# GAT tails that take both halves of the batches at once, and one output array: a four-layer graph network on one core

## The chip, the cores and the metric

The kernel runs on one core of a Trainium2 chip. A core has TensorE (PE, whose weight loads are listed as PEld), VectorE (DVE), ScalarE (ACT), GpSimd (POOL) and SyncE (SP), which work side by side, each through its own queue of instructions in order, and 16 DMA engines. The metric is the device time of one execution in microseconds (us); the median of several runs is quoted. Of one execution there is a profile: the start and length of every instruction, what ended the idle time before it, and the transfers.

## The reference

There are 8 batches of 2048 nodes with 128 features, and one adjacency matrix for all of them, with about 0.8% of its entries set. Four layers follow each other on the same x. Layers 0 and 1 are attention with 8 heads of 16 features over the neighbours, a residual and a layer norm, a feed-forward part of 256 and another residual and norm. The change doesn't touch these. Layers 2 and 3 are single-head graph attention (GAT):

```python
h = x @ W
e = leaky_relu(h @ a_src [:, None] + h @ a_dst [None, :], slope=0.2)
e = where(adj == 0, -inf, e)
out = softmax(e, axis=-1) @ h
y = out + x
x = ln_gamma * (y - mean(y)) * rsqrt(var(y) + 1e-5) + ln_beta
```

## The kernel before

**Tiles.** The nodes are sorted by the number of their neighbours and cut into 16 tiles of 128 nodes, one node per partition. Tile t handles up to 30, 23, 21, 20, 19, 18, 18, 17, 16, 16, 15, 14, 14, 13, 12, 11 neighbours per node, for t = 0 to 15. For each layer a table in DRAM holds one row per node with the projected features of all 8 batches and the attention terms (4 KB and a little more for layers 2 and 3). `gather` fetches one neighbour's row for each of a tile's 128 nodes with one indirect DMA that POOL issues (L320), so a tile of 20 neighbours takes 20 such instructions. They go to one of six buffers called kv, in chunks of 2 neighbours (layers 0 and 1) or 4 (layers 2 and 3).

**A chunk of a GAT layer** (`gat_chunk`). DVE makes the weights (L745, L746, L751) and multiplies the gathered rows of six batches by them (L757); ACT multiplies those of the last two batches (L762). DVE then adds the two halves of the chunk (L766), and PE accumulates the result in PSUM (L772). L766 needs both L757 and L762. After the last chunk of a tile, DVE divides by the sum of the weights and writes `o` (L649).

**The tail of a tile** (`gat_tail`). It runs twice per tile, once for batches 0 to 3 and once for batches 4 to 7. PE adds `o`, the residual and a constant row in PSUM (L782 to L790). `normed` then does the norm: ACT squares each batch's row and sums it up (L471), POOL raises the four sums of a node to the power of -0.5 (L476, 128 x 4 elements), and ACT scales by that (L480). The mean is taken out by the weights. For layer 2, PE transposes the result (L329), ACT copies it, and `project` makes the half row of layer 3's table, in a tile called rows. When the second half is done, `state_done` stores x and writes the 128 rows into the table with an indirect DMA from POOL (`put_rows`, L494), and counts it in `put`. For layer 3, DVE multiplies by gamma (L807) and adds beta (L808), and POOL writes the half tile to the output with an indirect DMA (L810, 256 KB). There are two output arrays, one for each four batches, which the host puts together.

**Order.** The order of the instructions on each engine is that in which the program emits them; no scheduler moves anything. `layers` goes through all chunks of all layers. For each chunk it calls `slot` three times, and a slot advances every running side thread and every tail by one step (to its next `yield`) and then lets `fetch` issue further gathers, up to 3 or 4 chunks ahead of the one at work. The two tails of a tile start 1 and 4 slots after `o` is written. So a tail's power lands in POOL's queue between the gathers of later chunks, and its squares and scales land in ACT's queue between the multiplies L762 of later chunks.

**Layer boundaries.** The gathers of a layer need the whole table, which the last tile of the layer before completes. To shorten that wait, the lists of tiles 0 and 1 are sorted so that some of their chunks need only the table without its last three, two or one tiles; `fetch` issues those as soon as `put` says so. A table write waits for the gathers of that table that are under way, and the gathers behind it wait for it to land.

**Buffers.** The half tiles of the norm are in a pool of two (tag n), the rows tile has one buffer, and the PSUM tiles of the tails come from a pool of three (`misc`).

Of the kernel before, what the change touches and what calls it, by code (L numbers as in the profile page):

```python
# [8 lines left out]
F32 = mybir.dt.float32  # L9
# [4 lines left out]
AF = mybir.ActivationFunctionType  # L14
# [68 lines left out]
def sparse_path(ctx: ExitStack, tc: tile.TileContext, ins: dict, out: bass.AP, flag: bass.AP):  # L83
# [19 lines left out]
    def misc():  # L103
        return pm.tile([P, 512], F32, tag="m", name="m")
# [12 lines left out]
    half = const.tile([P, 4], F32, name="half")  # L117
    nc.vector.memset(half, -0.5)

    spread = const.tile([P, P], F32, name="spread")  # L120
# [344 lines left out]
    def normed(z, dst):  # L465

        yield

        ss = small.tile([P, 4], F32, tag="ss", name="ss", bufs=3)
        for i in range(4):  # L470
            nc.scalar.activation(  # L471
                dst[:, i, :], z[:, i, :], AF.Square, bias=eps, scale=D**-0.5,
                accum_out=ss[:, i : i + 1],
            )
        rs = small.tile([P, 4], F32, tag="rs", name="rs", bufs=3)
        nc.gpsimd.tensor_tensor(rs, ss, half, op=ALU.pow)  # L476
        yield
        yield
        for i in range(4):
            nc.scalar.mul(dst[:, i, :], z[:, i, :], rs[:, i : i + 1])  # L480
        yield
# [18 lines left out]
    def project(l, i, xT, rows, t):  # L500

        w = W[l]
        if l < 2:
            for h in range(0, 4, 2):
                pp = misc().rearrange("p (b c) -> p b c", c=2 * D)
                if w["bias"] is not None:
                    nc.tensor.matmul(
                        pp, ones_bf, w["bias"][:, None, D:].to_broadcast([P, 2, 2 * D]),
                        start=True, stop=False, skip_group_check=True,
                    )  # L510
                for j in range(2):
                    nc.tensor.matmul(
                        pp[:, j, :], xT[:, i + h + j, :], w["qkv"][:, D:],
                        start=w["bias"] is None and j == 0, stop=True, skip_group_check=True,
                    )
                yield
                at = (i + h) * 2 * D
                nc.scalar.copy(rows[:, at : at + 512], pp.rearrange("p b c -> p (b c)"))  # L518
        else:
            pp = misc().rearrange("p (b c) -> p b c", c=D)  # L520
            nc.tensor.matmul(
                pp, ones_bf, w["bias"][:, None, :D].to_broadcast([P, 4, D]),
                start=True, stop=False, skip_group_check=True,
            )
# [22 lines left out]
            nc.scalar.copy(score[:, l - 2, t, 2 * i : 2 * i + 8], ps.rearrange("p b c -> p (b c)"))  # L547
# [106 lines left out]
    def rows_of(box):  # L654
        if "rows" not in box:
            box["rows"] = work.tile([P, NB * 2 * D], F32, tag="rows", name="rows", bufs=1)
        return box["rows"]
# [117 lines left out]
                )  # L775
        yield

    def gat_tail(l, t, box, i):
        wt = W[l]
        xT = box["x"]  # L780
        y = misc().rearrange("p (b c) -> p b c", c=D)
        nc.tensor.matmul(  # L782
            y, ones_bf, wt["row_z"][:, None, :].to_broadcast([P, 4, D]),
            start=True, stop=False, skip_group_check=True,
        )
        nc.tensor.matmul(
            y, ident, box["o"][:, i : i + 4, :], start=False, stop=False, skip_group_check=True
        )
        for j in range(4):
            nc.tensor.matmul(  # L790
                y[:, j, :], xT[:, i + j, :], wt["res1"], start=False, stop=True,
                skip_group_check=True,
            )
        n2 = work.tile([P, 4, D], F32, tag="n", name="n2")
        yield from normed(y, n2)
        if l == 2:
            pt = transpose4(n2)
            yield
            nc.scalar.copy(xT[:, i : i + 4, :], pt)
            yield  # L800
            yield from project(3, i, xT, rows_of(box), t)
            yield
            state_done(l, t, box)
        else:
            for _ in range(4):
                yield
            nc.vector.tensor_mul(n2, n2, last_g[:, None, :].to_broadcast([P, 4, D]))  # L807
            nc.vector.tensor_add(n2, n2, last_b[:, None, :].to_broadcast([P, 4, D]))  # L808
            yield
            nc.gpsimd.indirect_dma_start(  # L810
                out=out[i // 4],
                out_offset=bass.IndirectOffsetOnAxis(ap=perm[:, t : t + 1], axis=0),
                in_=n2.rearrange("p b d -> p (b d)"), in_offset=None,
            )
            state_done(l, t, box)


# [203 lines left out]
    for l in range(4):  # L1021
        per = 2 if l < 2 else 4
        for t, k, ns, folded in pieces(l, per):
# [2 lines left out]
            c["run"] = (attention_chunk if l < 2 else gat_chunk)(l, c)  # L1026
            every.append(c)
    now = [0, 0]

    def advance(group):  # L1030
        for g in list(group):
# [27 lines left out]
    def drain():  # L1059
        while threads or tails:  # L1060
# [93 lines left out]


@with_exitstack
def general_path(ctx: ExitStack, tc: tile.TileContext, ins: dict, outs: list):

# [444 lines left out]
    for b in range(B):  # L1603
        x = x_next
        if b + 1 < B:
            x_next = load_x(b + 1)
        attention(x, W[0])
        attention(x, W[1])
        gat(x, W[2])
        gat(x, W[3])  # L1610
        o = outs[b // 4][:, (b % 4) * D : (b % 4 + 1) * D]
        nc.sync.dma_start(o.rearrange("(t p) d -> p t d", p=P), x)


# [64 lines left out]
```

## Time and profile before

| what | us |
| --- | --- |
| median of 3 runs | 3421.49 |
| lowest and highest | 3416.98, 3424.4 |
| profiled execution | 3421.15 |
| its span | 3419.3 |
| DVE busy | 3063.5 (90%) |
| PE busy | 2746.3 (80%) |
| POOL busy | 2213.2 (65%) |
| ACT busy | 1429.0 (42%) |

The span is the time from the first to the last instruction; 1.85 us of the execution lie around it. The 16 DMA engines moved 986.52 MB, 289 GB/s on average. The four layers overlap little, and each has its own limits, so the shares over the whole span must not be read as those of the part in question. Layer 2 begins at about 2300 us and layer 3 at about 2840 us, and both are shorter than the layers before them. In a line of the groups, "out<-in" names the tiles, then comes the count, the busy time and the mean, and after the second bar the idle time of that engine just before these instructions and what ended it.

### The profile page before, as it was taken

Reading aid. Unit: us, or ns where it says so; the run is one execution under the profiler, and the core shown is the slowest. Engines: PE = TensorE matmul, PEld = TensorE weight load, DVE = VectorE, ACT = ScalarE, POOL = GpSimd, SP = SyncE. Lnnn points to the kernel's source line nnn. Section 1 sums busy time; section 2 is a strip of 40 time slices with the busy share of each in tenths; the row PEclk is TensorE's granted clock in tenths of the full one; section 3 lists DMA queues with packets and bytes.
Section 4 is the critical chain, followed back from the end, with each engine's and each line's share of the span. In section 5 each row is a group of like instructions: output and inputs, shape, how many; then the busy total and the mean of one; then the engine's idle time right before and its main releaser. Section 6 shows DMA issues by size and latency. Waiting matters only on the chain.

```text
span 3419.3 us, 34694 instructions
## 1 busy us (share of the span) xinstructions
PE 2746.3 (80%) x10618; PEld 1585.2 (46%) x10618; DVE 3063.5 (90%) x2727; ACT 1429.0 (42%) x4972; POOL 2213.2 (65%) x1501
## 2 busy tenths in 40 slices
PE   5647888888989997788888999985888976667775
PEld 4523445445555653455545555642444543233332
DVE  7789999999999989999999999965888876788885
ACT  5711333334444541233334344443555654344444
POOL 0065788688667655465676756646788865688873
PEclk9878999999999999999999999987999997889888
DMA  8487877888888777687887887757999986789883
GB/s 340 181 333 266 300 284 282 314 299 291 307 305 311 279 265 285 229 328 282 318 323 291 300 307 277 283 184 267 334 337 349 346 307 241 276 296 319 297 286 123
DMA packets 200881, 986.52 MB, mean 289 GB/s; under 512 B 32174, under 2 KB 33968, under 8 KB 128692
## 3 DMA queue, kind: packets, MB, share of 16 engines
q0 software_dynamic: 175280, 890.45, 71.8%
q1 hardware_dynamic: 20502, 75.52, 5.7%
q10 hardware_dynamic: 4904, 18.24, 1.4%
q8 instruction: 87, 1.43, 0.2%
q14 instruction: 108, 0.88, 0.1%
HBM read 937.16 MB, written 91.55 MB: 301 GB/s over the span
## 4 chain that ended last, share of the span: by engine, by line
DVE 34%; PE 23%; issue 18%; DMA 10%; POOL 6%; ACT 3%; POOLq 0%; DVEq 0%; ACTq 0%
DVE kv L620 12%; DVE kv L606 12%; PE acc L630 7%; PE acc L772 6%; DMA kv<-table,lists 5%; POOL kv L320 4%; DVE sc L609 2%; DVE kv L757 2%; DMA kv<-table,sorted_lists 2%; DVE kv L766 2%; PE m L712 2%; DVE sums L455 1%; DMA table<-rows,perm 1%; PE m L329 1%; PE m L691 1%
## 5 line engine op out<-in xcount | busy, mean ns | idle before, releaser
L320 POOL DMA_INDIRECT kv<-table,lists x955 | 1422.8, 1490 | 352.6 <-issue 205.8
L630 PE MATMUL acc<-kv,ident 128*128 128x512 f32 x2200 | 1107.2, 633 | 229.4 <-DVE kv L620 229.2
L772 PE MATMUL acc<-kv,ident 128*128 128x512 f32 x1184 | 618.2, 672 | 203.0 <-DVE kv L766 155.6
L630 PEld LDWEIGHTS acc<-kv,ident 128*128 128x128 f32 x2200 | 413.9, 202 | 663.1 <-issue 367.5
L606 DVE TENSOR_TENSOR kv<-kv,q 128x2048 f32<-128x2048 f32 (+1 forms) x282 | 629.4, 2232 | 18.9 <-DMA kv<-table,lists 10.1
L609 DVE TENSOR_REDUCE sc<-kv 128x128 f32<-128x2048 f32 (+1 forms) x284 | 634.0, 2233 | 9.2
L620 DVE TENSOR_TENSOR kv<-kv,w 128x2048 f32<-128x2048 f32 (+1 forms) x284 | 631.5, 2224 | 8.2 <-ACT w L615 7.4
L476 POOL TENSOR_TENSOR rs<-ss,half 128x4 f32<-128x4 f32 x192 | 290.5, 1513 | 422.6 <-ACT n L471 421.1
L471 ACT ACTIVATE n<-m,eps 128x128 f32<-128x128 f32 x768 | 271.9, 367 | 568.7 <-PE m L712 216.7
L772 PEld LDWEIGHTS acc<-kv,ident 128*128 128x128 f32 x1184 | 243.4, 216 | 508.2 <-issue 299.4
L757 DVE TENSOR_TENSOR kv<-kv,pair 128x3072 f32<-128x3072 f32 (+1 forms) x150 | 466.3, 3108 | 1.0
L766 DVE TENSOR_TENSOR kv<-kv 128x2048 f32<-128x2048 f32 (+1 forms) x150 | 296.2, 1975 | 147.3 <-ACT kv L762 147.3
L762 ACT ACTIVATE kv<-kv,ws 128x128 f32<-128x128 f32 x1108 | 339.4, 406 | 146.3 <-DVE ws L751 118.9
L480 ACT ACTIVATE n<-m,rs 128x128 f32<-128x128 f32 x768 | 219.6, 370 | 371.5 <-POOL rs L476 371.2
L615 ACT ACTIVATE w<-sc,lmask 128x64 f32<-128x64 f32 x554 | 164.9, 351 | 457.6 <-DVE sc L609 457.0
L320 POOL DMA_INDIRECT kv<-table,sorted_lists x153 | 199.9, 1307 | 114.5 <-PE acc L630 47.6
L494 POOL DMA_INDIRECT table<-rows,perm x57 | 106.5, 1868 | 110.2 <-ACT rows L518 26.4
L329 PE MATMUL m<-ident,n 128*128 128x128 f32 x640 | 106.9, 289 | 85.3 <-ACT n L480 85.3
L471 ACT ACTIVATION_READ_ACCUMULATOR n<-m,eps 128x1 f32 x768 | 157.4, 205 | 0.0
L712 PE MATMUL m<-w_L_w,hT 128*128 128x128 f32 x1024 | 156.4, 275 | 0.0
L329 PEld LDWEIGHTS m<-ident,n 128*128 128x128 f32 x640 | 81.5, 146 | 142.2 <-ACT n L480 92.7
L712 PEld LDWEIGHTS m<-w_L_w,hT 128*128 128x128 f32 x1024 | 135.2, 192 | 0.0
(234 smaller groups left out, 3237.8 us busy)
## 6 DMA issues: line engine op xcount, KB each, us to landing
kept<-xT SPq DMA_DIRECT2D x48, 512.0 KB, 7.6
xT<-kept SPq DMA_DIRECT2D x48, 512.0 KB, 6.4
kv<-in_adj_dram SPq DMA_DIRECT2D x16, 1024.0 KB, 6.4
table<-kv ACTq DMA_DIRECT2D x16, 1024.0 KB, 4.3
kv<-table,lists POOLq DMA_INDIRECT x955, 7.0
kv<-in_x_nodes_dram SPq DMA_DIRECT2D x16, 512.0 KB, 6.6
kv<-table,sorted_lists POOLq DMA_INDIRECT x153, 6.2
found<-cand POOLq DMA_DIRECT2D x16, 64.0 KB, 4.1
```

The costliest lines, as they stand in the source:

```text
L320: nc.gpsimd.indirect_dma_start(out=dst, out_offset=None, in_=tables[l][:, :], in_offset=bass.IndirectOffsetOnAxis(ap=index, axis=0), bound ...
L471: nc.scalar.activation(dst[:, i, :], z[:, i, :], AF.Square, bias=eps, scale=D**-0.5, accum_out=ss[:, i : i + 1],)
L476: nc.gpsimd.tensor_tensor(rs, ss, half, op=ALU.pow)
L606: nc.vector.tensor_mul(kk, kk, q[:, None].to_broadcast([P, ns, NB, D]))
L609: nc.vector.tensor_reduce(sc[:, :ns].rearrange("p s (b h) -> p (s b) h", h=NH), kk.rearrange("p s b (h j) -> p (s b) h j", h=NH), axis=AX. ...
L620: nc.vector.tensor_mul(vv, vv, w[:, k : k + ns, :].rearrange("p s (b h) -> p (s b) h", h=NH)[:, :, None, :] .to_broadcast([P, ns * NB, HD, ...
L630: nc.tensor.matmul(acc[:, j, :], merge if c["folded"] else ident, kv[:, i, 4 * j : 4 * j + 4, D:], start=k + i == 0, stop=c["last"] and i ...
L712: nc.tensor.matmul(y[:, j, :], hT[:, f, j, :], wt["2"][:, f, :], start=False, stop=f == 1, skip_group_check=True,)
L757: nc.vector.tensor_mul(hv[:, :, :nv, :], hv[:, :, :nv, :], wc[:, :, :nv, None].to_broadcast([P, ns, nv, D]))
L762: nc.scalar.mul(hv[:, i, b, :], hv[:, i, b, :], ws[:, i, b - nv : b - nv + 1])
L766: nc.vector.tensor_add(hv[:, : ns - left], hv[:, : ns - left], hv[:, left:ns])
L772: nc.tensor.matmul(acc[:, j, :], merge if c["folded"] else ident, hv[:, i, 4 * j : 4 * j + 4, :], start=k + i == 0, stop=c["last"] and i = ...
```

## The change

A GAT tail now takes both halves. It adds both in PSUM, squares the first half, squares the second, and calls one power of 128 x 8 elements. In layer 2 the halves then go on one by one, the second two slots behind the first, to the same table write. In layer 3 both halves are written into the tile that was the table's rows (one buffer), gamma and beta are applied to all 128 x 1024 elements in one instruction each, and one indirect DMA of 512 KB writes them to one output array of 2048 rows of 8 x 128; the host transposes it. The steps between are laid out anew in slots. Besides, `slot` advances the tails a second time in every third slot as long as the chunk at work is one of the last tile of layer 2, or is one of layers 2 or 3 whose table is not yet complete. Layers 0 and 1 keep their own tails with a power of 128 x 4, and are affected only in that `half` is now 8 wide.

```diff
-    def gat_tail(l, t, box, i):
+    def gat_tail(l, t, box):
         wt = W[l]
         xT = box["x"]
...
-        n2 = work.tile([P, 4, D], F32, tag="n", name="n2")
-        yield from normed(y, n2)
+        if l == 2:
+            ns = [work.tile([P, 4, D], F32, tag="n", name="n2") for _ in range(2)]
+        else:
+            n = rows_of(box)[:, : B * D].rearrange("p (b d) -> p b d", d=D)
+            ns = [n[:, :4, :], n[:, 4:, :]]
+        ys = [None, None]
+        ss = small.tile([P, 8], F32, tag="ss", name="ss", bufs=3)
+        rs = small.tile([P, 8], F32, tag="rs", name="rs", bufs=3)
...
+        def half_rows(h):
+            scaled(h)
+            yield
+            pt = transpose4(ns[h])
+            yield
+            nc.scalar.copy(xT[:, 4 * h : 4 * h + 4, :], pt)
+            yield
+            yield from project(3, 4 * h, xT, rows_of(box), t)
+            yield
+            state_done(l, t, box)
+
+        added(0)
+        yield
+        squares(0)
+        added(1)
+        yield
+        squares(1)
+        nc.gpsimd.tensor_tensor(rs, ss, half, op=ALU.pow)
+        for _ in range(3):
+            yield
         if l == 2:
-            pt = transpose4(n2)
-            yield
-            nc.scalar.copy(xT[:, i : i + 4, :], pt)
-            yield
-            yield from project(3, i, xT, rows_of(box), t)
-            yield
-            state_done(l, t, box)
+            parts = [half_rows(0), later(2, lambda: half_rows(1))]
+            while parts:
+                advance(parts)
+                yield
         else:
-            for _ in range(4):
-                yield
-            nc.vector.tensor_mul(n2, n2, last_g[:, None, :].to_broadcast([P, 4, D]))
-            nc.vector.tensor_add(n2, n2, last_b[:, None, :].to_broadcast([P, 4, D]))
+            scaled(0)
+            yield
+            scaled(1)
+            for _ in range(3):
+                yield
+            nc.vector.tensor_mul(n, n, last_g[:, None, :].to_broadcast([P, B, D]))
             yield
+            nc.vector.tensor_add(n, n, last_b[:, None, :].to_broadcast([P, B, D]))
+            yield
             nc.gpsimd.indirect_dma_start(
-                out=out[i // 4],
-                out_offset=bass.IndirectOffsetOnAxis(ap=perm[:, t : t + 1], axis=0),
-                in_=n2.rearrange("p b d -> p (b d)"), in_offset=None,
+                out=out, out_offset=bass.IndirectOffsetOnAxis(ap=perm[:, t : t + 1], axis=0),
+                in_=n.rearrange("p b d -> p (b d)"), in_offset=None,
             )
             state_done(l, t, box)
...
+    def hurry():
+        c = every[min(now[0], len(every) - 1)]
+        return c["l"] == 2 and c["t"] == NT - 1 or c["l"] > 1 and put[c["l"]] < NT
+
     def slot():
         advance(threads)
         advance(tails)
         fetch()
+        beat[0] += 1
+        if beat[0] % 3 == 0 and hurry():
+            advance(tails)
...
-        part = attention_tail if l < 2 else gat_tail
-        tails.append(later(1, lambda: part(l, t, box, 0)))
-        tails.append(later(4, lambda: part(l, t, box, 4)))
+        if l < 2:
+            tails.append(later(1, lambda: attention_tail(l, t, box, 0)))
+            tails.append(later(4, lambda: attention_tail(l, t, box, 4)))
+        else:
+            tails.append(later(1, lambda: gat_tail(l, t, box)))
```

The inner functions `added`, `squares` and `scaled` hold the same instructions as the tail and `normed` did, for half h.

More of the change, by code (lines that the diff above doesn't have):

```diff
@@ L116, in sparse_path @@
     nc.vector.memset(onesc, 1.0)
-    half = const.tile([P, 4], F32, name="half")
+    half = const.tile([P, 8], F32, name="half")
     nc.vector.memset(half, -0.5)
@@ L475, in normed @@
         rs = small.tile([P, 4], F32, tag="rs", name="rs", bufs=3)
-        nc.gpsimd.tensor_tensor(rs, ss, half, op=ALU.pow)
+        nc.gpsimd.tensor_tensor(rs, ss, half[:, :4], op=ALU.pow)
         yield
@@ L776, in gat_chunk, with added @@
         yield
-    def gat_tail(l, t, box, i):
+    def gat_tail(l, t, box):
         wt = W[l]
         xT = box["x"]
[L781 to L789, printed above, removed]
-            nc.tensor.matmul(
-                y[:, j, :], xT[:, i + j, :], wt["res1"], start=False, stop=True,
+        if l == 2:
[6 more added lines that the diff above has]
+        rs = small.tile([P, 8], F32, tag="rs", name="rs", bufs=3)
+        def added(h):
+            ys[h] = y = misc().rearrange("p (b c) -> p b c", c=D)
+            nc.tensor.matmul(
+                y, ones_bf, wt["row_z"][:, None, :].to_broadcast([P, 4, D]),
+                start=True, stop=False, skip_group_check=True,
+            )
+            nc.tensor.matmul(
+                y, ident, box["o"][:, 4 * h : 4 * h + 4, :], start=False, stop=False,
@@ L792, in gat_tail, with squares @@
                 skip_group_check=True,
             )
-        n2 = work.tile([P, 4, D], F32, tag="n", name="n2")
-        yield from normed(y, n2)
-        if l == 2:
-            pt = transpose4(n2)
+            for j in range(4):
+                nc.tensor.matmul(
+                    y[:, j, :], xT[:, 4 * h + j, :], wt["res1"], start=False, stop=True,
+                    skip_group_check=True,
+                )
+        def squares(h):
+            for j in range(4):
+                nc.scalar.activation(
+                    ns[h][:, j, :], ys[h][:, j, :], AF.Square, bias=eps, scale=D**-0.5,
+                    accum_out=ss[:, 4 * h + j : 4 * h + j + 1],
+                )
@@ L798, in gat_tail, with scaled @@
+        def scaled(h):
+            for j in range(4):
+                at = 4 * h + j
+                nc.scalar.mul(ns[h][:, j, :], ys[h][:, j, :], rs[:, at : at + 1])
+        def half_rows(h):
+            scaled(h)
             yield
-            nc.scalar.copy(xT[:, i : i + 4, :], pt)
+            pt = transpose4(ns[h])
             yield
-            yield from project(3, i, xT, rows_of(box), t)
+            nc.scalar.copy(xT[:, 4 * h : 4 * h + 4, :], pt)
+            yield
+            yield from project(3, 4 * h, xT, rows_of(box), t)
@@ L802, in gat_tail @@
             yield
             state_done(l, t, box)
-        else:
-            for _ in range(4):
+        added(0)
[7 more added lines that the diff above has]
+            yield
+        if l == 2:
+            parts = [half_rows(0), later(2, lambda: half_rows(1))]
+            while parts:
+                advance(parts)
+                yield
+        else:
+            scaled(0)
+            yield
+            scaled(1)
+            for _ in range(3):
@@ L1028, in sparse_path @@
     now = [0, 0]
+    beat = [0]
     def advance(group):
@@ L1156, in general_path @@
 @with_exitstack
-def general_path(ctx: ExitStack, tc: tile.TileContext, ins: dict, outs: list):
+def general_path(ctx: ExitStack, tc: tile.TileContext, ins: dict, out: bass.AP):
     nc = tc.nc
@@ L1610, in general_path @@
         gat(x, W[3])
-        o = outs[b // 4][:, (b % 4) * D : (b % 4 + 1) * D]
+        o = out[:, b * D : (b + 1) * D]
         nc.sync.dma_start(o.rearrange("(t p) d -> p t d", p=P), x)
@@ L1663 @@
         ).ap()
-    outs = [
-        nc.dram_tensor(f"out_{i}_dram", [N, 4 * D], F32, kind="ExternalOutput").ap()
-        for i in range(B // 4)
-    ]
+    out = nc.dram_tensor("out_dram", [N, B * D], F32, kind="ExternalOutput").ap()
     with tile.TileContext(nc) as tc:
@@ L1670 @@
             flag = fp.tile([1, 1], I32, name="flag")
-            sparse_path(tc, aps, outs, flag)
+            sparse_path(tc, aps, out, flag)
             bad = nc.values_load(flag[:1, :1], min_val=0, max_val=P)
             with tc.If(bad > 0):
-                general_path(tc, aps, outs)
+                general_path(tc, aps, out)
     r = run_bass_kernel_spmd(nc, [arrays], core_ids=[0])
-    got = r.results[0]
-    halves = [got[f"out_{i}_dram"].reshape(N, 4, D).transpose(1, 0, 2) for i in range(B // 4)]
-    return np.ascontiguousarray(np.concatenate(halves, axis=0))
+    got = r.results[0]["out_dram"]
+    return np.ascontiguousarray(got.reshape(N, B, D).transpose(1, 0, 2))
```

## The prediction

> **What bounds the kernel now.** I first split the span into the stretches that the change touches, then read for each what GpSimd (POOL) does, then who waits for it. The windows view, cut by hand at the layer boundaries (columns: stretch, its length, busy time of PE, PEld, DVE, ACT, POOL, granted clock, DMA share, GB/s):
>
> ```profile
> 2210.00:2350.00 140.00, 99.53 (x453) 62.30 (x451) 81.28 (x68) 62.96 (x236) 64.76 (x56) 0.85 0.54 190
> 2350.00:2770.00 420.00, 358.50 (x1356) 201.60 (x1357) 358.19 (x383) 234.65 (x924) 339.18 (x273) 0.94 0.95 343
> 2770.00:2900.00 130.00, 84.56 (x311) 47.80 (x310) 82.22 (x81) 55.07 (x216) 70.53 (x58) 0.80 0.69 243
> 2900.00:2975.00 75.00, 48.15 (x119) 21.50 (x117) 56.14 (x63) 24.80 (x96) 49.77 (x40) 0.86 0.80 280
> 2975.00:3350.00 375.00, 267.18 (x650) 120.21 (x650) 320.48 (x359) 172.53 (x653) 300.28 (x237) 0.87 0.88 300
> ```
>
> These are the boundary from layer 1 to 2, layer 2's steady part, the boundary from 2 to 3, layer 3's first tiles and its steady part. Layers 0 and 1 before them are not edited. At the boundaries everything is half idle. In layer 2 the DMA share is 0.95, so at most 5% of 420, 21 us, can be won there. Layer 3 has slack on every engine at first sight. The groups of instructions on POOL in that last window (count, busy us, mean ns, idle before):
>
> ```profile
> L320 POOL DMA_INDIRECT kv<-table,lists x192 | 244.4, 1273 | 56.1 <-issue 39.0 <-PE acc L772 7.5 <-DMA kv<-table,lists 3.4
> L810 POOL DMA_INDIRECT out_dram<-n,perm x22 | 33.2, 1509 | 6.7 <-issue 4.0 <-DVE kv L757 1.2 <-DVE ws L751 0.6
> L476 POOL TENSOR_TENSOR rs<-ss,half 128x4 f32<-128x4 f32 x23 | 25.6, 1114 | 18.0 <-ACT n L471 17.7
> ```
>
> POOL is idle 375 - 300.28 = 74.7 us, but 17.7 of that is the power waiting for squares, and nearly all the rest is 0.2 to 0.3 us between two instructions. It hardly waits for a free buffer: its queue is always full. The waits of the same window (total, times, longest):
>
> ```profile
> ACT n L480 <- POOL rs L476: 83.9, 23, 11.6
> DVE kv L766 <- ACT kv L762: 57.9, 17, 10.0
> ACT n L471 <- DMA out_dram<-n,perm: 45.7, 10, 9.2
> ```
>
> DVE, busy 320 of 375, waits for one thing only: the multiplies that ACT does for two batches (L762). These stand in ACT's queue behind the scaling (L480), which waits for the power, which stands in POOL's queue among gathers. So the loop is: full POOL queue, late power, late ACT, late DVE. A POOL instruction saved is worth its time until DVE's 57.9 us are gone. The timeline of POOL in the first tiles of layer 3 and at the boundary before it shows two other places:
>
> ```profile
> 2951.35 1.03 POOL L810 DMA_INDIRECT out_dram<-n,perm  x1 [0.30 <-issue]
> 2958.54 1.04 POOL L476 TENSOR_TENSOR rs<-ss,half 128x4 f32<-128x4 f32 x1 [6.17 <-ACT n L471]
> ...
> 2966.83 1.03 POOL L810 DMA_INDIRECT out_dram<-n,perm  x1 [0.30 <-issue]
> 2973.99 1.03 POOL L476 TENSOR_TENSOR rs<-ss,half 128x4 f32<-128x4 f32 x1 [6.13 <-ACT n L471]
> ```
>
> ```profile
> 2812.54 1.05 POOL L494 DMA_INDIRECT table<-rows,perm  x1 [5.95 <-DMA kv<-table,sorted_lists]
> ...
> 2821.71 1.05 POOL L476 TENSOR_TENSOR rs<-ss,half 128x4 f32<-128x4 f32 x1
> ...
> 2863.33 2.96 POOL L494 DMA_INDIRECT table<-rows,perm  x1 [9.79 <-ACT score L547]
> ```
>
> In the first, a power waits for squares that wait for a scatter of the output to land, because they write the tile it reads. In the second, tile 14's second power starts at 2821.71 although its squares ended at 2811.4 (ACT's timeline): it stands behind four gathers, which wait for the table write of 2812.54 to land. The table's last write, 2863.33, opens layer 3.
>
> **What the Trainium skill says.** "SBUF — State Buffer", section "Who interferes with whom": a DVE instruction with two SBUF inputs contends with a GpSimd instruction that reads SBUF, and whoever is first holds the port pair throughout. The trace agrees:
>
> ```profile
> 3067.55 2.28 DVE L766 TENSOR_TENSOR kv<-kv 128x2048 f32<-128x2048 f32 x1
> 3067.65 3.10 POOL L320 DMA_INDIRECT kv<-table,lists  x1 [0.30 <-issue]
> ```
>
> A gather takes 1.00 us alone (3065.01) and 3.10 here. Hence the means above 1.0, and each POOL instruction removed can also take a collision with it. "DMA: Bandwidth & Descriptors", section "Anatomy of one DMA — SWDGE (gpsimd) path", prices a transfer at 2.0 us plus bytes at 436 GB/s: 2.6 us for 256 KB, 3.2 for 512 KB. The trace is slower, 5.2 us median from issue to landing for the 256 KB scatter; I keep its 5.2 and add 256 KB at the 343 GB/s seen, 0.75. "GPSIMD Engine Reference", section "3.1 Elementwise — side-by-side cycle accounting", gives about 2.6 cycles per element for a two-input operation. Four more columns would then cost an estimated 0.01 us; but the page does not price a power, and the trace has 1.04 us for four columns where a one-column memset takes 0.10. So the page is no guide here.
>
> **The change, part by part.** The unknown is the power of 128x8. Lower bound 1.04 us (all fixed), upper bound 0.10 + 2 x 0.94 = 2.0 (all but the memset's 0.10 grows with the columns). I take the middle, 1.5. The squares, scales, adds and projections keep their number (8 squares take 2 x 1.45 = 2.9 us, 8 scales 2 x 1.14 = 2.3). The two halves of the scatter become one of 512 KB with the same 128 rows, so I keep 1.5 us for its issue on POOL.
>
> 1. Boundary 1 to 2. Now the second power of tile 13 (2290.15) stands behind eight gathers that waited for the write at 2275.84, and ACT waits 7.71 us for it. The instruction order has a merged power ahead of the next table write, and the extra advance of the tails brings it earlier. Later work of tile 14 fills part. Gain 5 us, bounds 0 and 12.
>
> 2. Layer 2, 13 tiles in the window. Two powers with their gaps, 2 x (1.12 + 0.2) = 2.64, become 1.5 + 0.2: 0.94 each, 12 us of POOL (bounds 0.44 and 1.4 each: 6 and 18). DMA at 0.95 covers part. I take half, 6 us, bounds 0 and 16.
>
> 3. Boundary 2 to 3. Tile 14's only power now follows the table write of tile 13 directly, near 2813.7, against 2821.71. The next table write, at 2836.87 before (15.2 behind that power, partly waiting for tile 15's first power ahead of it), comes near 2828. It lands in 4.2 us; eight gathers at 1.3 follow, then tile 15's power near 2843.3, 1.5 us, then scale, transpose, project as before (11.5 us; 2852.49 to 2863.33 was 10.8). The last write is at 2856.3 instead of 2863.3: gain 7, bounds 2 and 13.
>
> 4. First tiles of layer 3. Two stalls of 6.17 and 6.13 become one. The order puts no gather between tile 0's scatter and tile 1's power, so POOL waits 6.15 + 0.75 (bigger transfer) + 1.45 (four more squares) = 8.4. Saved 12.3 - 8.4 = 3.9, plus 1.1 + 1.5 + gaps in POOL work: 6 us, bounds 0 and 10.
>
> 5. Layer 3's steady part, 11 tiles. Before, per tile, 2 x (1.11 + 0.2) + 2 x (1.51 + 0.3) = 6.25 us of POOL; after, 1.7 + 1.81 = 3.5. Saved 2.74 x 11 = 30 (25 to 35 over the power's bounds). DVE has 32 fewer instructions here but the same elements: 2 x (0.69 + 0.69) against one pair of doubled width, nothing. The give-back: the layer's result now lives in the single "rows" tile, so the next tile's squares wait for the scatter to land: 5.95 + 2.9 = 8.9 us behind the scatter before its power can run. By the order, two or three chunks of gathers (over 10 us) lie between for the tiles up to 7, which hides it; for the five pairs 7 to 12 only one chunk of 3 or 4 (5.9 us with the scatter) does: 3.0 x 5 = 15. The old wait of 17.7 goes. Net POOL 30 + 17.7 - 15 = 33. But behind the squares wait ACT's L762, and behind those DVE: part of its 57.9 remains. I take 18, bounds -25 and 45 (DVE's and the DMA's room: 375 - 320 and 12% of 375).
>
> 6. End. The last three tiles' tails now follow each other through one tile: scatter, landing, 8 squares, power, 8 scales, multiply and add of 1.4 each, scatter. Before, the halves overlapped and the last two scatters stood at 3408.72 and 3411.91. The longer link costs 1.45 + 0.5 + 1.1 + 1.4 = 4.4 per tile, less the halves' own staggering (3.2). Loss 2 us, bounds 0 and 8.
>
> Sum: -5 - 6 - 7 - 6 - 18 + 2 = -40. The profiled execution took 3421.15 us (span 3419.3 and 1.85 around it), 0.3 below the median of the runs shown, 3421.49: 3421 - 40 = 3381.
>
> **The rivals.**
> (B) The savings in the steady parts are hidden: DMA at 0.95 in layer 2, and in layer 3 ACT's wait for the landing replaces its wait for the power, so DVE idles as before. Only 1, 3, 4 and 6 remain: -16, 3405. For it: DVE never waits for a gather in layer 3. Against: POOL's full queue.
> (C) Slower: the single rows tile. Place: ACT's queue in layer 3's late tiles. If the squares' wait for the landing holds up L762 as long as at 2977.97, where DVE lost 9.98 us, and in all 14 tiles, DVE loses 14 x 10 = 140 against 58 now, less about 45 of POOL's saving used meanwhile and 16 at the boundaries: +21, 3442. It decides once DVE's wait over these tiles passes 58 + 45 + 16 = 119, 8.5 us per tile against 5 now. Against: 2 or 3 chunks lie between in most tiles.
> (D) All of DVE's wait in both layers goes and the power is all fixed: -5 - 16 - 13 - 10 - 45 + 2 = -87, 3334.
> (E) The extra advance brings nothing, as the boundaries are bound by landings: parts 1 and 3 are nil, -28, 3393; it lies within the main case's range.
>
> **How the numbers follow.** Main case (with E) 0.47, B 0.26, C 0.15, D 0.12. About 0.2%, 7 us, is what a measurement of this kernel can tell from no change. Faster: main 0.46, B 0.22, D 0.12 = 0.80; same: 0.01 + 0.04 + 0.01 = 0.06; slower 0.14, from C. The range leaves out the lower half of D and the upper part of C: 3347 to 3425; the main case alone would be 3362 to 3400.
>
> **What would show it.** Right: the power of eight columns between 1.04 and 2.0 us; half as many powers and scatters in layers 2 and 3; the last table write near 2856; one stall of 8 us at layer 3's first tiles; DVE's wait for L762 below 58 us and the window of layer 3 about 18 us shorter. Wrong: ACT's squares waiting for the output's scatter much over 46 us and DVE's idle time growing with it (C), or both unchanged (B).

## The result and the profile after

| kernel | median us | lowest to highest | ratio to before, 95% interval |
| --- | --- | --- | --- |
| before | 3419.85 | 3415.67 to 3426.47 | |
| changed | 3406.51 | 3401.1 to 3409.74 | 0.996 [0.9948, 0.9973] |

The change is faster by 13 us. 40 were forecast: the sign held, and the size was three times too big. The profiled execution of the changed kernel has a span of 3402.8 us, 16.5 less than before. 7.0 of these are there by the time layer 1 writes its last `o`, before any edited instruction. The other traces below reach that point between 2248.4 and 2259.3 us, so I take the 7.0 for a difference between executions; that the wider `half` has a part in it is not excluded.

To see where the rest came from, I take from both traces the times at which DVE starts to write a tile's `o` (L649), and subtract. "End" is the last scatter of the output.

| stretch | before | changed | difference | forecast |
| --- | --- | --- | --- | --- |
| layer 1, last `o`, to layer 2, tile 13 | 507.9 | 501.2 | -6.7 | -11 (steps 1 and 2) |
| layer 2, tile 13, to layer 3, tile 0 | 150.8 | 156.3 | +5.5 | -7 |
| layer 3, tile 0 to 2 | 76.6 | 67.8 | -8.9 | -6 |
| layer 3, tile 2 to 13 | 358.9 | 356.8 | -2.1 | -18 |
| layer 3, tile 13, to the end | 60.9 | 65.0 | +4.1 | +2 |
| behind the last scatter | 7.4 | 5.9 | -1.5 | 0 |

It matters where the time is divided. Counted from layer 1's last `o`, the changed kernel is 8.2 us ahead of before at layer 2's tile 1, 3.9 behind at tile 2, 6.7 ahead at tile 13, 14.7 ahead at tile 14 and 9.0 behind at tile 15. So single tiles of layer 2 swing by more than the gain in question, and I divide at tile 13, near the end of the forecast's window for layer 2.

So 16 us were gained up to tile 13 and in layer 3's first tiles, and 10 lost at the boundary and the end; layer 3's steady part, where nearly half of the gain was expected, gave almost nothing. The windows of the changed kernel, with the bounds used for before:

```profile
2350.00:2770.00 420.00, 365.61 (x1386) 204.07 (x1384) 364.40 (x391) 239.62 (x940) 334.25 (x255) 0.95 0.95 343
2770.00:2900.00 130.00, 82.90 (x282) 45.85 (x282) 76.97 (x78) 52.48 (x200) 74.68 (x59) 0.80 0.70 243
2900.00:2975.00 75.00, 51.39 (x124) 22.65 (x124) 60.95 (x65) 31.62 (x120) 55.22 (x41) 0.86 0.82 289
2975.00:3350.00 375.00, 271.97 (x680) 124.56 (x680) 322.52 (x342) 166.33 (x643) 287.75 (x211) 0.86 0.87 301
```

In the last line POOL has 26 instructions and 12.5 us of work less than before, and DVE is no busier (322.52 against 320.48). POOL's groups in that window, and then the waits of all engines and those of DVE:

```profile
L320 POOL DMA_INDIRECT kv<-table,lists x188 | 256.7, 1366 | 56.1 <-issue 39.4 <-PE acc L772 7.4 <-DMA kv<-table,lists 4.9
L836 POOL TENSOR_TENSOR rs<-ss,half 128x8 f32<-128x8 f32 x11 | 18.9, 1717 | 20.3 <-ACT rows L809 20.1
L854 POOL DMA_INDIRECT out_dram<-rows,perm x12 | 14.2, 1184 | 3.7 <-issue 3.0 <-ACT kv L762 0.3 <-DMA kv<-table,lists 0.3
```

```profile
ACT rows L809 <- DMA out_dram<-rows,perm: 78.0, 10, 13.2
...
ACT rows L817 <- POOL rs L836: 41.7, 6, 13.5
```

```profile
DVE kv L766 <- ACT kv L762: 25.2, 5, 7.5
DVE rows L850 <- ACT rows L817: 19.8, 10, 4.9
```

The powers and scatters are half as many, as meant, and took 33 us where they took 59. But ACT's wait for the scatter to land rose from 45.7 to 78.0, and POOL still waits for squares, 20.1 where it was 17.7. DVE's wait for L762 fell from 57.9 to 25.2, and 19.8 of that came back as a wait of the gamma multiply (L850) for the scales. In layer 3's tiles 2 to 13 DVE is idle for 51.7 us, as before (51.3).

Half of what the powers and scatters saved was also taken back by POOL's gathers: 256.7 us for 188, where 192 took 244.4. A gather that starts while DVE adds the two halves of a chunk (L766, both inputs in SBUF) takes much longer than one that starts in the multiply before it (L757, whose weights lie in PSUM):

```profile
3213.96 3.35 DVE L757 TENSOR_TENSOR kv<-kv,pair 128x3072 f32<-128x3072 f32 x1
...
3214.93 1.00 POOL L320 DMA_INDIRECT kv<-table,lists  x1 [0.30 <-PE acc L772]
...
3216.24 1.00 POOL L320 DMA_INDIRECT kv<-table,lists  x1 [0.31 <-issue]
...
3217.23 2.28 DVE L766 TENSOR_TENSOR kv<-kv 128x2048 f32<-128x2048 f32 x1
...
3217.54 2.84 POOL L320 DMA_INDIRECT kv<-table,lists  x1 [0.30 <-issue]
```

The multiply by gamma and the addition of beta, with both inputs in SBUF, act like L766. Between tiles 2 and 13, 13 gathers started in one of their instructions of 0.69 us before, and took 1.3 us on average; after the change 22 started in those of 1.22 us, two per tile, and took 1.6. No run here separates this from the rest.

One of the late tiles, in the timeline of all engines:

```profile
3220.69 1.01 POOL L854 DMA_INDIRECT out_dram<-rows,perm  x1 [0.30 <-issue]
...
3227.75 0.37 ACT L809 ACTIVATE rows<-m,eps 128x128 f32<-128x128 f32 x1 [11.28 <-DMA out_dram<-rows,perm]
...
3230.51 1.88 ACT L762 ACTIVATE kv<-kv,ws 128x128 f32<-128x128 f32 x6
3230.80 1.67 POOL L836 TENSOR_TENSOR rs<-ss,half 128x8 f32<-128x8 f32 x1 [4.00 <-ACT rows L809]
3232.42 1.23 DVE L766 TENSOR_TENSOR kv<-kv 128x1024 f32<-128x1024 f32 x1 [3.32 <-ACT kv L762]
```

The scatter starts at 3220.69, lands 7 us later, and only then may ACT write the next tile's squares into the same rows. ACT has been idle for 11.28 us, of which some 8 are due to the scatter, as PE had the first half of the sums ready at about 3219.9; L762 is queued behind the squares, and DVE and POOL wait for ACT.

At the boundary from layer 2 to 3 (the timeline of POOL, to be held against the times 2812.54 to 2863.33 of before), and in layer 3's first tiles:

```profile
2803.94 1.01 POOL L494 DMA_INDIRECT table<-rows,perm  x1 [7.36 <-DMA kv<-table,sorted_lists]
2804.97 1.67 POOL L836 TENSOR_TENSOR rs<-ss,half 128x8 f32<-128x8 f32 x1
...
2839.88 1.67 POOL L836 TENSOR_TENSOR rs<-ss,half 128x8 f32<-128x8 f32 x1
2855.12 2.36 POOL L494 DMA_INDIRECT table<-rows,perm  x1 [13.56 <-ACT score L547]
```

```profile
2944.12 1.01 POOL L854 DMA_INDIRECT out_dram<-rows,perm  x1 [0.30 <-issue]
2953.54 1.67 POOL L836 TENSOR_TENSOR rs<-ss,half 128x8 f32<-128x8 f32 x1 [8.41 <-ACT rows L809]
```

The single stall of 8.41 us is the 8.4 of the forecast. The last table write, 2855.12, also came near the forecast 2856, but by luck: counted from layer 1's last `o` it is only 1.2 us earlier than before (605.4 against 606.6), where step 3 alone promised 7, and steps 1 to 3 together 18.

### The profile page after: what moved, and what is told of

Its sections match the earlier page's. It is cut to its first block, busy times and chain, and to the rows that moved or that the text cites. A ratio compares the mean times of both kernels' runs of the same rounds, so it can differ in the third digit from the quotient of the medians.

```text
span 3402.8 us, 34669 instructions
## 1 busy us (share of the span) xinstructions
PE 2743.1 (81%) x10618; PEld 1582.9 (47%) x10618; DVE 3058.3 (90%) x2695; ACT 1426.6 (42%) x4972; POOL 2207.9 (65%) x1453
## 4 chain that ended last, share of the span: by engine, by line
DVE 32%; PE 25%; issue 18%; DMA 10%; POOL 5%; ACT 3%; POOLq 0%; DVEq 0%; ACTq 0%
DVE kv L620 11%; DVE kv L606 11%; PE acc L630 8%; PE acc L772 6%; DMA kv<-table,lists 4%; POOL kv L320 3%; DMA kv<-table,sorted_lists 3%; DVE sc L609 2%; PE m L712 2%; DVE kv L766 2%; DMA table<-rows,perm 2%; DVE kv L757 2%; PE m L329 2%; DVE sums L455 1%; DMA out_dram<-rows,perm 1%
## 5 line engine op out<-in xcount | busy, mean ns | idle before, releaser
L320 POOL DMA_INDIRECT kv<-table,lists x955 | 1450.0, 1518 | 357.2 <-issue 206.7
L630 PEld LDWEIGHTS acc<-kv,ident 128*128 128x128 f32 x2200 | 413.7, 202 | 655.1 <-issue 367.5
L757 DVE TENSOR_TENSOR kv<-kv,pair 128x3072 f32<-128x3072 f32 (+1 forms) x150 | 466.1, 3108 | 1.0
L476 POOL TENSOR_TENSOR rs<-ss,half 128x4 f32<-128x4 f32 x128 | 221.2, 1728 | 325.4 <-ACT n L471 324.6
L766 DVE TENSOR_TENSOR kv<-kv 128x2048 f32<-128x2048 f32 (+1 forms) x150 | 296.0, 1974 | 129.0 <-ACT kv L762 129.0
L762 ACT ACTIVATE kv<-kv,ws 128x128 f32<-128x128 f32 x1108 | 339.0, 406 | 163.7 <-DVE ws L751 105.5
L471 ACT ACTIVATE n<-m,eps 128x128 f32<-128x128 f32 x512 | 181.0, 366 | 427.1 <-PE m L712 217.4
L480 ACT ACTIVATE n<-m,rs 128x128 f32<-128x128 f32 x512 | 146.0, 370 | 109.4 <-POOL rs L476 109.0
L691 PE MATMUL m<-n1T,w_L_gnn_W 128*128 128x512 f32 x256 | 131.5, 597 | 0.8 <-ACT n1T L686 0.4
```

The source lines that it names most:

```text
L320: nc.gpsimd.indirect_dma_start(out=dst, out_offset=None, in_=tables[l][:, :], in_offset=bass.IndirectOffsetOnAxis(ap=index, axis=0), bound ...
L476: nc.gpsimd.tensor_tensor(rs, ss, half[:, :4], op=ALU.pow)
L630: nc.tensor.matmul(acc[:, j, :], merge if c["folded"] else ident, kv[:, i, 4 * j : 4 * j + 4, D:], start=k + i == 0, stop=c["last"] and i ...
L757: nc.vector.tensor_mul(hv[:, :, :nv, :], hv[:, :, :nv, :], wc[:, :, :nv, None].to_broadcast([P, ns, nv, D]))
L762: nc.scalar.mul(hv[:, i, b, :], hv[:, i, b, :], ws[:, i, b - nv : b - nv + 1])
L766: nc.vector.tensor_add(hv[:, : ns - left], hv[:, : ns - left], hv[:, left:ns])
```

## The experiments

Two theories stood at the start. "New waits": POOL's time does set the pace of layers 2 and 3, and what was saved was given back by waits that the change itself makes. "Bound": DVE and the transfers set it, and POOL's time never counted. All ratios are to the kernel before, on the same chip.

**Two tiles for the result.** Odd tiles of layer 3 use another tile, which is free by then, so that no squares wait for a scatter to land.

```diff
-            n = rows_of(box)[:, : B * D].rearrange("p (b d) -> p b d", d=D)
+            if t % 2:
+                n = work.tile([P, B, D], F32, tag="xn", name="xs", bufs=1)
+            else:
+                n = rows_of(box)[:, : B * D].rearrange("p (b d) -> p b d", d=D)
```

> Layer 3's results of odd tiles go to a second tile that is free there, so a tile's squares no longer wait for the previous tile's scatter to land. Theory 'new waits' (what POOL saved in layer 3 was given back by waits that the change made: ACT for the landing, 65.7 us in the window of layer 3, and DVE for the scales, 20 us): ACT's wait for the landing goes, POOL's 20 us of waiting for squares shrinks to under 8, DVE's wait for L762 falls below 25, and the time is 8 to 15 us below the changed kernel, ratio to before 0.992 to 0.994. Rival 'DVE and DMA are the bound' (POOL's time never set layer 3's pace): the waits go, but the ratio stays at 0.996.

Measured: 3369.32 us, ratio 0.9846 [0.9829, 0.9864], 37 us below the changed kernel and far more than "new waits" expected. ACT's wait for the landing is gone, and in 2890 to 3330 POOL waits 3.4 us for squares where it was 28.5. The stretches show where the time went: layer 3's tiles 2 to 13 took 333.7 us instead of 356.8, tiles 0 to 2 took 59.5 instead of 67.8, and the end 57.8 instead of 65.0. "Bound" falls. The new tile's size or place is not a cause, since it only alternates with the old one.

**The gamma multiply later**, on top of the two tiles, so that DVE should meet it with the scales done.

```diff
             scaled(1)
-            for _ in range(3):
+            for _ in range(5):
                 yield
```

> As the run with two result tiles, and the multiply by gamma is emitted two slots later, so that DVE doesn't meet it before the scales are done. Theory 'new waits': DVE's 20 us of waiting for the scales in layer 3 goes too, another 5 to 12 us, ratio 0.989 to 0.992. Rival 'DVE and DMA are the bound': as the run with two result tiles, within 3 us.

Measured: 3367.78 us, 0.985 [0.9835, 0.9864]; no different. DVE's wait for the scales (28.4 us in 2890 to 3330 with the two tiles) was not worth anything by itself: DVE waits for L762 again instead (25.5 us there). A part of "new waits" falls here. This wait shows that DVE came early; it was no cause.

**No extra advance** of the tails at the boundaries.

```diff
-        beat[0] += 1
-        if beat[0] % 3 == 0 and hurry():
-            advance(tails)
```

> The extra advance of the tails at the boundaries is taken away, all else as in the changed kernel. Theory 'the extra advance hurts at the boundary from layer 2 to 3' (there the changed kernel lost some 5 us against before): about 5 us better there, 2 worse at the boundary from 1 to 2, ratio 0.995. Rival 'it is what gains at both boundaries' (as predicted, 12 us): 8 to 12 us worse, ratio 0.999. Third, it moves nothing that counts: 0.996.

Measured: 3398.58 us, 0.9934 [0.9919, 0.9949], 8 us better than the changed kernel. From layer 2's tile 13 to layer 3's tile 0 it took 144.6 us instead of 156.3 (before: 150.8), while up to tile 13 nothing changed (501.9 and 501.2). POOL's timeline at the boundary names the reason:

```profile
2800.64 1.67 POOL L836 TENSOR_TENSOR rs<-ss,half 128x8 f32<-128x8 f32 x1
2809.43 1.06 POOL L494 DMA_INDIRECT table<-rows,perm  x1 [7.12 <-DMA kv<-table,sorted_lists]
```

Here tile 14's power is ahead of tile 13's table write. In the changed kernel (above) the order is reversed: the advance moves the table write forward, it waits 7.36 us at the head of POOL's queue for the gathers under way, and the power stands behind it. With the power, ACT waits, and DVE behind ACT; the waits from 2765 to 2865, first in the changed kernel, then here:

```profile
DVE kv L766 <- ACT kv L762: 40.7, 7, 10.8
...
ACT n L817 <- POOL rs L836: 30.7, 3, 13.0
```

```profile
DVE kv L766 <- ACT kv L762: 13.0, 4, 7.0
ACT n L817 <- POOL rs L836: 11.3, 1, 11.3
```

A part of this is only moved: in the same window DVE waits 24.0 us for layer 3's gathers here, and in the changed kernel not yet (7.1 us just behind it). But the last table write comes 9.2 us sooner, counted from the same point in layer 1.

**Layer 2's part alone**: the kernel before, with the merged tail in layer 2 and the extra advance; layer 3 keeps its two half tails and two output arrays. Only the choice between the tails is shown; it stands in place of the changed kernel's, and the old tail and the old output arrays are put back.

```diff
+        if l == 2:
+            tails.append(later(1, lambda: gat_tail2(l, t, box)))
+        else:
+            part = attention_tail if l < 2 else gat_tail
+            tails.append(later(1, lambda: part(l, t, box, 0)))
+            tails.append(later(4, lambda: part(l, t, box, 4)))
```

> The kernel before with the merged tail in layer 2 and the extra advance only; layer 3 keeps its two half tails, two powers and two scatters into two arrays. Theory 'new waits': the edits of layer 2 and the boundaries alone are worth 4 (boundary 1 to 2) + 5 (layer 2) - 5 (boundary 2 to 3) = 4 us, and layer 3's part the other 9, ratio 0.999. Rival: all of the gain comes from layer 2 and the boundaries, and layer 3's part brings nothing: ratio 0.996.

Measured: 3415.64 us, 0.9987 [0.998, 0.9993]: 4 us, as "new waits" said. By the stretches it is less: 5.2 us gained up to layer 2's tile 13 (502.7), where 9 were expected, and 3.6 lost from there to layer 3's tile 0 (154.4), where 5 were.

**Two tiles and no advance together**, then from there **two powers** or **two scatters** again.

```diff
-        nc.gpsimd.tensor_tensor(rs, ss, half, op=ALU.pow)
+        nc.gpsimd.tensor_tensor(rs[:, :4], ss[:, :4], half[:, :4], op=ALU.pow)
+        nc.gpsimd.tensor_tensor(rs[:, 4:], ss[:, 4:], half[:, 4:], op=ALU.pow)
```

```diff
-            nc.gpsimd.indirect_dma_start(
-                out=out, out_offset=bass.IndirectOffsetOnAxis(ap=perm[:, t : t + 1], axis=0),
-                in_=n.rearrange("p b d -> p (b d)"), in_offset=None,
-            )
+            for h in range(2):
+                nc.gpsimd.indirect_dma_start(
+                    out=out[h], out_offset=bass.IndirectOffsetOnAxis(ap=perm[:, t : t + 1], axis=0),
+                    in_=ns[h].rearrange("p b d -> p (b d)"), in_offset=None,
+                )
...
```

> The changed kernel with two result tiles in layer 3 and without the extra advance. If the two causes are independent, 37 us and 8 us below the changed kernel: 3361, ratio 0.983. If an earlier layer 3 only meets the landing waits elsewhere: as with two result tiles alone, 0.985.

> As the run with two result tiles and no extra advance, but two powers of 128x4 one behind the other in place of one of 128x8; all else at its place. A power of 8 columns takes 1.72 us, one of 4 columns 1.04 to 1.12, so POOL gets 0.5 us more of work per tile and a gap of 0.2, 20 us in all over 28 tiles. Theory 'POOL's time sets the pace of layers 2 and 3': 10 to 20 us slower than that run. Rival 'the gain comes from the order of the merged tail, in which ACT waits once for both halves': within 3 us of it.

> As the run with two result tiles and no extra advance, but the result leaves by two scatters of 256 KB into two output arrays. POOL gets 1.2 + 0.3 us more per tile of layer 3, 15 to 24 us in all. Theory 'POOL's time sets the pace': 10 to 20 us slower than that run. Rival 'order of the merged tail': within 3 us.

Measured on one chip: 3387.08 (0.9893 [0.9879, 0.9907]), 3382.51 (0.9878 [0.9862, 0.9894]) and 3401.93 (0.9935 [0.9922, 0.9947]). The first was 26 us above what the two separate gains promised (22 by the ratios), and the second was not slower than the first but 4.6 us faster, which neither theory allows. So these comparisons could not be taken as they stood. The first's layer 3 was as fast as it should be (332.0 us for tiles 2 to 13), but its layer 2, tiles 2 to 14, took 361.9 us, with the same instructions that took 338.3 on the chip before; in the second it took 354.4, and in the third, with the first's instructions, 367.5. The windows of the two kernels in layer 2, first the one on this chip, then the same one on a third chip:

```profile
2450.00:2550.00 100.00, 80.17 (x281) 45.16 (x280) 81.32 (x81) 51.47 (x200) 72.46 (x58) 0.88 0.91 317
```

```profile
2450.00:2550.00 100.00, 86.62 (x318) 47.22 (x317) 87.59 (x91) 56.69 (x220) 81.22 (x63) 0.95 0.96 347
```

TensorE was granted 0.88 instead of 0.95, and POOL waited for buffers that PE still read, 25.4 us between 2440 and 2750, where it was 4.8 on the third chip:

```profile
POOL kv L320 <- PE acc L772: 25.4, 14, 8.2
```

So four kernels were run again side by side on that third chip.

> The changed kernel once more, beside the next three on one chip, since the run with two result tiles and no extra advance went on another chip than the runs it is compared with, and its layer 2, whose instructions it shares with them, took 24 us longer there at a lower granted clock (0.88 against 0.95 in 2450 to 2550). Expected: ratio 0.996 on whichever chip.

> Two result tiles, with the extra advance. Theory 'the chip made the difference': on one chip this is 5 to 8 us slower than the run without the extra advance. Rival 'with two result tiles the extra advance is of use': it stays 15 us or so faster than that.

> Two result tiles, no extra advance. Theory 'the chip made the difference': ratio 0.982 to 0.984, layer 2 from its third tile to its fifteenth in 338 us as in the other runs. Rival: 0.989 and a layer 2 of 360 us again, whatever the chip.

> Two powers of 128x4 in place of one of 128x8, on the same chip as the run before this. Theory 'POOL's time sets the pace': layer 3 from its third tile to its fourteenth 8 us longer, as in the first comparison, layer 2 some 8 us longer, together 10 to 20 us slower. Rival: layer 2 does not care, since the transfers set its pace there: 8 us slower.

| kernel | median us | ratio, 95% interval | layer 1 to layer 2, 13 | to layer 3, 0 | layer 3, 0 to 2 | 2 to 13 | end |
| --- | --- | --- | --- | --- | --- | --- | --- |
| changed | 3406.45 | 0.996 [0.9945, 0.9976] | 502.0 | 156.5 | 67.2 | 357.9 | 66.2 |
| two tiles | 3366.9 | 0.9851 [0.9837, 0.9865] | 501.5 | 153.3 | 59.4 | 333.1 | 57.9 |
| two tiles, no advance | 3354.26 | 0.9824 [0.9805, 0.9844] | 504.1 | 145.0 | 58.3 | 332.7 | 58.1 |
| the same, two powers | 3366.45 | 0.9848 [0.9833, 0.9862] | 504.4 | 144.9 | 59.9 | 340.2 | 55.0 |

The two gains add up, within a few microseconds: the single tile cost 40 us, the advance 12.6 more by the medians and 7 by the stretches (8.3 at the boundary, 2.6 lost before it); the rest is there before the first edited instruction, as a difference between executions. Without both, the change is worth 64 us on this chip (53 to 67 by the interval), and this is the fastest kernel of the study.

Two powers cost 12 us by the medians and 6.3 by the stretches. Up to layer 3's tile 0 they cost nothing (649.2 against 649.1 us), in its first tiles 1.5, in tiles 2 to 13 7.5 (8.6 on the other chip), and at the end they gain 3.1. So of the two theories POOL's time sets the pace in layer 3, and the rival was right for layer 2. Two scatters cost 15 us in layer 3's tiles 2 to 13 (347.1 against 332.0, on the other chip). Counted with the gathers that collide, POOL was busy there for 273.8 us with one power and 282.5 with two, and on the other chip for 273.3 with one scatter and 286.0 with two. So 8.7 us of POOL cost 7.5, and 12.7 cost 15: a microsecond of POOL in layer 3 is worth about one of the time. Why that one chip grants less clock in layer 2 was not found.

**The wait for the landing in the kernel before.** There each square waited for the scatter two halves back. Four halves instead of two are in use here:

```diff
-        n2 = work.tile([P, 4, D], F32, tag="n", name="n2")
+        if l == 3 and i:
+            n2 = work.tile([P, NB, D], F32, tag="q", name="q")[:, :4, :]
+        else:
+            n2 = work.tile([P, 4, D], F32, tag="n", name="n2")
```

> The kernel before, where only layer 3's second halves take another pair of tiles that is free there, so that four halves instead of two are in use and no square waits for a scatter to land (45.7 us of ACT's time in the window of layer 3). Theory 'the wait for the landing costs whatever the tail looks like': 10 to 20 us faster than before, ratio 0.994 to 0.997. Rival 'it costs only where the whole tile hangs on it, as in the changed kernel': within 3 us of before, ratio 0.999 to 1.001.

Measured: 3403.98 us against 3426.19, 0.9941 [0.9929, 0.9953], 22 us, a little above the range expected. It is 12.0 in layer 3's tiles 0 to 2, 6.0 in tiles 2 to 13 (352.9), 3.7 at the end. This nearly closes the account of tiles 2 to 13, although its terms come from different chips: 358.9 before, less 6.0 for the landing, 15.0 for the second scatter and 7.5 for the second power makes 330.4; 332.7 was measured with all three gone. So about a third of the 64 us above is not owed to the merge: more buffers would have given it to the kernel before.

## Why the prediction was wrong

The steps that failed are step 5, in the size of its give-back, and step 3, in its sign.

1. Boundary from 1 to 2 (-5 forecast): the gain came and went. Layer 2's tile 1 is 8.2 us earlier, and tile 2 is 3.9 later again. Between the two, ACT waits 7.2 us for a table write to land before it may fill the single `rows` tile, which it did not do before. That looks like layer 3's wait for its scatter, but no run tests it. The extra advance does nothing here (502.0 and 501.5 us to tile 13 with it, 501.9 and 504.1 without).

```profile
ACT rows L541 <- DMA table<-rows,perm: 7.2, 1, 7.2
```

2. Layer 2 (-6): steps 1 and 2 together are -6.7 at tile 13, where -11 was forecast. The step lived on POOL's time, and that was hidden: two powers in place of one change nothing at tile 13 (504.4 against 504.1). What is gained after tile 2 has another source, probably the order of the merged tail. In 2440 to 2750 ACT waited for a power 20 times before, 89.7 us in all, and 11 times, 66.6 us, with two tiles and no advance; with two powers one behind the other it is still 11 times and 68.7. DVE's wait for L762 falls from 35.4 to 21.6, and is 19.9 with two powers. So ACT stops once per tile, with all squares behind it, rather than twice. This is argued and not isolated. TensorE's granted clock is a rival that no run separates: over tiles 2 to 13 it was 0.95 before and 0.96 to 0.97 with the merged tail. On the chip where it fell to 0.90 to 0.93 with the merged tail, that tail took 522.7 to 532.8 us to tile 13, and the tail of before 511.0 at 0.94.

3. Boundary from 2 to 3 (-7, measured +5.5): wrong in the sign. The power of tile 14 was where the forecast put it, right behind a table write, and tile 14's write was indeed 16 us earlier on the trace's clock (2820.58 against 2836.87, with the 7.0 from layer 1 in it). The step did not count that ahead of the power stands a write that must wait for the gathers, and that ACT and DVE wait along with the power. Without the extra advance, which brings the write forward, the boundary gains 6.2 us (144.6), and 5.8 with two tiles (145.0), near the forecast. The advance alone cost 11.7 and 8.3. Rival E, too, had it that the advance is at worst of no use.

4. First tiles (-6, measured -8.9): right, with the stall of 8.4 us as it was worked out. What the step did not see is that the stall need not be there.

5. Layer 3 (-18, measured -2.1): this is the step that failed most. Its gross term was right: POOL's powers and scatters got shorter by 25 us and some gaps, 30 were forecast, and a microsecond of POOL is worth about one. The give-back was mis-sized: 15 us forecast for five pairs of tiles, counted as idle time of POOL. With two result tiles the stretch is 23 to 25 us shorter, so that is what the wait for the landing cost. The wait stands in ACT's queue, where L762 is behind it, so DVE loses with POOL; and the scatter of 512 KB takes 6.6 us to land (median), not 5.95. The forecast named this as the slower rival's mechanism, and let it decide only from 8.5 us of DVE's waiting per tile. DVE waited about 4 us per tile in the changed kernel's window (25.2 and 19.8 over eleven), and the time was lost all the same, since it is lost against what the saving would have brought, not against before.

A second term was put at nothing: "the same elements" on DVE. The forecast expected fewer collisions of DVE and POOL. But in every tile two gathers start in the wide gamma and beta instructions and take 1.6 us, and the gathers of tiles 2 to 13 took 246.8 us in all instead of 231.0. The rule that the forecast itself quotes, of two inputs in SBUF, would have told which instructions of DVE to look at.

6. End (+2, measured +4.1): right in sign. The single tile's part is 8 us (66.2 against 57.9), so the rest of the change gains there.

The power of eight columns took 1.67 us at least and 1.72 on average in the changed kernel's window, inside the bounds of 1.04 and 2.0 and above the middle of 1.5; with two tiles and no advance the average was 2.1 in layer 3's tiles 2 to 13. The time of 3406.5 is near the 3405 of rival B, in which the savings of the steady parts are hidden. For the steady parts that rival was right: the second power is hidden in layer 2, and in layer 3 ACT's wait for the landing took the place of its wait for the power (83.9 us before, 41.7 after), with DVE idle as before. But in layer 3 the saving was real and spent, as the two tiles show, and the 12 us that the rival still counted on at the boundaries did not come; that its number was met is in part luck.

## What to carry to other kernels

Before two results are merged into one tile, ask who writes that tile next and what stands behind the writer in its queue: a single buffer that a DMA still reads stops a whole in-order engine until the transfer has landed. Bringing a chain forward in a queue also brings forward its waits; an instruction that waits for transfers under way must not get ahead of one that others need now. And what an engine saves is to be counted with what its other instructions then cost: here the gathers took back half of it.

## What the runs showed of the hardware

A power on GpSimd grows with the columns: 1.04 us for 128x4 and 1.67 for 128x8, so an estimated 0.16 per column on top of 0.41, from these two widths alone. An indirect scatter of 128 rows occupies POOL for about 1.0 us whether a row has 2 or 4 KB (minima of 0.96 and 1.01), and lands after 5.2 and 6.6 us in the median. A gather issued on POOL takes about 1.0 us. In the changed kernel's window from 2975, 40 started in DVE's addition L766, whose inputs both lie in SBUF, and took 2.35 us on average; 94 started in the multiply L757, which reads one input from PSUM, and took 1.00 us.

The same instructions of layer 2, tiles 2 to 14, took 338 us on two chips and 362 on a third, where TensorE's granted clock was 0.88 instead of 0.95 in a part of it, while layer 2 in its form before took 357.9 us there and 356.8 elsewhere; so what the merged tail gains there depends on the chip.
